# Ring depths of the one-hot and message tiles, and the iteration in which a block's end reads TensorE's results, in a two-layer graph attention and mixture-of-experts kernel

## The chip, the cores and the metric

The kernel runs on one core of one Trainium2 chip. The metric is the device time of one execution in microseconds (us); for a kernel with several runs the median is given. A core has five engines with their own instruction streams: TensorE (PE, with its weight loads shown apart as PEld), VectorE (DVE), ScalarE (ACT), GpSimd (POOL) and SyncE (SP). They wait for each other on semaphores. Here POOL issues the row gathers, SP nearly all other transfers.

## The reference, cut to what matters

There are N = 6250 nodes with 256 features and E = 206250 edges, sorted by `dst`. Two graph attention layers are followed by a mixture of 8 experts, each with a residual. A layer is

```
h = x @ W.T + b
score = (h @ a[:d])[src] + (h @ a[d:])[dst]
e = exp(-leaky_relu(score, 0.2))
h_prime = segment_sum(e[:, None] * h[dst], src, num_segments=N)
h_prime = layernorm(h_prime) * g + beta        # then elu
```

Layer 1 has 8 heads of 64 columns (512 in all), layer 2 one head of 256. The expert part takes a layernorm of the result, a router with the top 2 of 8, and for each expert `gelu(t @ w1 + b1) @ w2 + b2`, weighted and added.

## The kernel before, in words

**Stages.** First the edges are sorted into 49 blocks of 128 source nodes, while the table of layer 1 (`tab1`, a row of 512 features and 8 scores for each node) is made. Then `edges` runs layer 1, with `middle` closing each block into a row of `tab2` (256 features and a score); then `edges` runs layer 2, with `tail` closing each block and feeding the experts. A last branch, for graphs that overflow the block capacity, is not taken with these inputs.

**Groups.** A block's edges are handled in groups of GT = 5 tiles of 128 edges: 7 groups in a block, 6 in the last, so 342 groups in a layer. `edges` emits an order written out by hand. Iteration t of its loop (L587) emits, for different groups, the seven stages of the list at L579; "ahead" is how many groups before its use a stage is emitted:

- `weigh`, group t+2, on DVE: reduce the source scores from a PSUM bank `ps` into `ssum` (L541), add the gathered scores (L543), leaky relu into `lr` (L489); ACT makes `ee` of it (L490).
- `messages`, group t+1, on DVE. In layer 1 it makes `hot`, 5 one-hot matrices of 128 by 128 (L556), and `msg`, the gathered rows times `ee` (L559). In layer 2 it makes only `hot`, with `ee` multiplied in (L565, five instructions), and the gathered tile `gt` itself serves as the message.
- `source_sums`, group t+4, on PE: five small matmuls of the one-hot rows `ot` into `ps` (L536).
- `add`, group t, on PE: five matmuls of `hot` and message into the block's accumulator `acc` (L574). In f32 the profile shows each as two matmuls and two weight loads, so 10 matmul records a group.
- `one_hot`, group t+5, on DVE: `ot` (L530).
- `sources`, group t+11, on SP: the transfer of `rb` (L519).
- `gather`, 6 groups ahead in layer 1 and 8 in layer 2, on POOL: five indirect transfers into `gt` (L525).

An engine executes its own instructions in this order, so an instruction that waits holds up everything behind it on its engine.

**Rings.** A tile with `bufs=n` is written anew for group m once the last reader of group m-n is done. Before: `hot` 3, `msg` 3, `ot` 3, `gt` 6 (layer 1) or 8 (layer 2), `rb` 6, and in PSUM `ps` 2, `acc` 2, `ee` 2 and one bank `mid` in layer 1. Thus `hot` of group m waits for `add` of group m-3; `ps` of group m is made by PE once `weigh` of group m-2 has read the bank; a gather into layer 1's `gt` waits for `messages`, in layer 2 for `add`.

**Block ends.** When `add` has emitted the last group of a block at iteration t, a generator is put on the list `running` with t+2 (L596); from then on each iteration advances it to its next `yield`, after the stages of that iteration. In layer 1 its steps are: mean and centring on DVE, squares on ACT (L673 to L678); variance (L681, L682) and its root; scaling and transposes of PE into `pt2` (L685 to L690); nothing; ACT reads `pt2` (L696, L698); DVE makes `ht` (L702) and PE multiplies it into `ph2` (L705) in the same step; nothing; DVE adds the bias out of `ph2` into `row2` (L709) and SP stores it (L710). `pt2`, `ph2` and the transposes `pe` of `read_back` (L478 to L484) share the bank `mid`. In layer 2 (`tail`) the transposes of step 3 (L798) are copied by ACT two steps later (L801), the router product (L805) is read by DVE two steps after it was emitted (L809).

**Read-back.** Every 21 groups of layer 1 `read_back` loads the sorted edges of three later blocks and makes their indices; it is started at iterations with t % 21 == 0 (L588) and runs as a generator too.

Of the kernel before, what the change touches and what calls it, by code (L numbers as in the profile page):

```python
# [29 lines left out]
P = 128  # L30
ALPHA = 0.2
EPS = 1e-5
TILES = 35
GT = 5
# [12 lines left out]
def kernel(ctx: ExitStack, tc: tile.TileContext, x, src, dst, w_heads, b_heads, a_heads,  # L47
# [30 lines left out]
    RBL = 3  # L78
# [19 lines left out]
    def bank(tag, name):  # L98
        return banks["pool"].tile([P, 512], F32, tag=tag, name=name, bufs=banks["bufs"][tag])
# [392 lines left out]
    def edges(es, layer, table, sel, k, width, block_done, more=None):  # L492
# [11 lines left out]
        groups = [(b, g) for b in range(NB) for g in range(tiles[b] // GT)]  # L504
        now = [{} for _ in groups]
        accs = {}

        def tile_of(n, name, shape, bufs, dtype=F32):
            now[n][name] = eb.tile(shape, dtype, name=name, bufs=bufs)
            return now[n][name]  # L510

        def where(n):
            b, g = groups[n]
            return b, b // RBL, (b % RBL) * PITCH + g * GT
# [35 lines left out]
        def messages(n):  # L550
            b, c, t0 = where(n)
            gt, ee = now[n]["gt"], now[n]["ee"]
            hot = tile_of(n, "hot", [P, GT, P], 3)
            sl = sloc[c][:, t0:t0 + GT]
            if k > 1:
                nc.vector.tensor_tensor(hot, iota_ps[:, None, :P].to_broadcast([P, GT, P]),  # L556
                                        sl[:, :, None].to_broadcast([P, GT, P]), op=OP.is_equal)
                msg = tile_of(n, "msg", [P, GT, width], 3)
                nc.vector.tensor_mul(msg.rearrange("p j (h d) -> p j h d", h=k),  # L559
                                     gt[:, :, :width].rearrange("p j (h d) -> p j h d", h=k),  # L560
                                     ee[:, :, :, None].to_broadcast([P, GT, k, width // k]))
            else:
                now[n]["msg"] = gt
                for j in range(GT):
                    nc.vector.tensor_scalar(hot[:, j, :], iota_n, sl[:, j:j + 1], ee[:, j, :],  # L565
                                            op0=OP.is_equal, op1=OP.mult)

        def add(n):
# [8 lines left out]
            return b if g == last else None  # L577

        stages = [(weigh, 2), (messages, 1), (source_sums, 4), (add, 0), (one_hot, 5), (sources, 5 + RB), (gather, GB)]  # L579
        running = []  # L580
        t = -5 - RB
        with tc.manual_schedule():
            if layer == 1:
                for _ in read_back(eb, 0):
                    pass
                running.append((t, read_back(eb, 1)))
            while t < len(groups) or running or (more and more(len(groups))):  # L587
                if layer == 1 and 0 <= t < len(groups) and t % (RBL * TILES // GT) == 0:  # L588
                    c = groups[t][0] // RBL + 2
                    if c < NCH:  # L590
                        running.append((t, read_back(eb, c)))
                for stage, ahead in stages:
                    if 0 <= t + ahead < len(groups):
                        b = stage(t + ahead)
                        if b is not None:
                            running.append((t + 2, block_done(b, accs.pop(b)[:, :width])))  # L596
                for of in list(running):
                    if of[0] <= t and next(of[1], True):
                        running.remove(of)
                if more and t < len(groups):  # L600
                    more()
                t += 1
# [64 lines left out]
    def middle(ms):  # L667
        mw = ms.enter_context(tc.tile_pool(name="mid_w", bufs=2))

        def block_done(b, acc):  # L670
# [29 lines left out]
            yield  # L700

            nc.vector.scalar_tensor_tensor(ht, ex, 1.0, ht, op0=OP.min, op1=OP.add)  # L702
            ph = bank("mid", "ph2")
            for k in range(KH):
                nc.tensor.matmul(ph[:, :C2], ht[:, k, :], wo[:, k, :], start=(k == 0), stop=(k == KH - 1))  # L705
            yield
            yield
            row = mw.tile([P, C2], F32, name="row2")
# [6 lines left out]
    def tail(ts):  # L715
# [49 lines left out]
        def block_done(b, acc):  # L765
# [32 lines left out]
                nc.tensor.transpose(pt[:, k * P:(k + 1) * P], tok[:, k * P:(k + 1) * P], ident)  # L798
            yield
            yield  # L800
            nc.scalar.copy(tokt[:, :, i * P:(i + 1) * P], pt[:, :F].rearrange("p (k n) -> p k n", k=KF))  # L801
            yield
            pl = bank("pt", "pl")
            for k in range(KF):
                nc.tensor.matmul(pl[:, :NE], tokt[:, k, i * P:(i + 1) * P], rws[:, k, :],  # L805
                                 start=(k == 0), stop=(k == KF - 1))
            yield
            yield
            nc.vector.tensor_copy(logits[:, i, :], pl[:, :NE])  # L809
# [122 lines left out]
        def more(steps=None):  # L932
# [11 lines left out]
            return some  # L944

        return block_done, more


    with ExitStack() as es:
        psum_of("first", es, acc=2, ps=2, ee=2, mid=1, iota=1)  # L950
        edges(es, 1, tab1, sel1, H, HD, middle(es))
        pieces(es.enter_context(tc.tile_pool(name="sel2", bufs=1)), sel2, s2, 1)

    with ExitStack() as es:
        psum_of("second", es, acc=2, ps=2, ffn=3, pt=1)
        done, more = tail(es)
        edges(es, 2, tab2, sel2, 1, F, done, more)
# [70 lines left out]
```

## Time and profile before

| | |
|---|---|
| five runs, us | 5814.6, 5835.68, 5831.93, 5821.91, 5812.93 |
| median, us | 5821.91 |
| the profiled execution, us | 5818.56 |
| its span from first to last instruction, us | 5816.8 |
| mean granted TensorE clock | 0.825 |
| busy share: PE, DVE, POOL, ACT | 72%, 57%, 60%, 22% |
| edges' sort and table, about | 0 to 490 us |
| layer 1, about | 490 to 3160 us |
| layer 2 with the experts, about | 3210 to 5710 us |
| last experts, about | 5710 to 5817 us |

The busy time of an engine by itself does not say what bounds the kernel: the three large ones rest between 28% and 43% of the time, and within a stage they hand work to each other in rings. So the views to read are those of one stage: which wait ends last, and who was waited for. In a timeline the columns are the start and the duration in us, the engine, the line and operation, the tiles, the count of merged instructions, and in brackets the idle time just before with what ended it. "issue" there stands for a wait that no recorded event explains on the engine's own side, "remote" for one that no recorded event of another engine explains.

### The profile page before, as it was taken

The numbers are of one execution on the slowest core, as the hardware profiler recorded it, in microseconds if no ns is written. First come the engines' busy times: TensorE is split into PE (matmuls) and PEld (weight loads), VectorE is DVE, ScalarE is ACT, GpSimd is POOL, SyncE is SP. The second block draws the span as 40 slices with busy tenths as digits, with TensorE's granted clock in tenths as the row PEclk, the third lists the DMA queues.
The fourth block names the chain that finished last, engine by engine and source line by source line (L and its number), as shares of the span: only waits on it lengthen the run. The fifth ranks groups of instructions, "written<-read, shape, count | busy, mean of one in ns | idle before, by whom it ended". The sixth has DMA issues, their size and how long they took to land.

```text
span 5816.8 us, 55830 instructions
## 1 busy us (share of the span) xinstructions
PE 4182.6 (72%) x17929; PEld 2507.9 (43%) x17929; DVE 3300.0 (57%) x8062; ACT 1289.4 (22%) x2363; POOL 3463.4 (60%) x3570
## 2 busy tenths in 40 slices
PE   5784677776777677777767356787778777777778
PEld 4662333333333333333333234555555545555555
DVE  7874666666666666666666244444444444445443
ACT  1110111111111111111111012333334333333433
POOL 2335666666666566665664666666666666666660
PEclk8896888888878888888888667888888888888889
DMA  2115666666666666666664544444444444444440
GB/s 73 57 42 147 193 195 196 196 190 194 192 195 198 193 195 196 195 198 189 193 201 140 149 117 116 121 121 116 120 122 113 121 121 122 114 121 123 113 114 17
DMA packets 381489, 847.54 MB, mean 146 GB/s; under 512 B 90125, under 2 KB 209732, under 8 KB 381186
## 3 DMA queue, kind: packets, MB, share of 16 engines
q0 software_dynamic: 223232, 682.22, 41.8%
q1 hardware_dynamic: 150340, 155.05, 9.5%
q10 hardware_dynamic: 7614, 6.62, 0.4%
q8 instruction: 142, 2.33, 0.2%
q14 instruction: 161, 1.32, 0.1%
HBM read 814.41 MB, written 29.16 MB: 145 GB/s over the span
## 4 chain that ended last, share of the span: by engine, by line
PE 33%; DVE 20%; issue 18%; another core or an unknown queue 11%; POOL 10%; DMA 7%; DVEq 0%; ACT 0%; POOLq 0%; ACTq 0%; SPq 0%
PE acc L574 19%; POOL gt L525 10%; DVE msg L559 8%; PE ph L882 5%; PE py L890 5%; DMA srt<-run,to 5%; DMA gt<-tab,dst_idx 2%; DVE hot L565 2%; DVE hot L556 1%; DVE ot L530 1%; PE ps L536 1%; DVE ssum L541 1%; DVE ssum L543 1%; PE ph L705 1%
## 5 line engine op out<-in xcount | busy, mean ns | idle before, releaser
L525 POOL DMA_INDIRECT gt<-tab,dst_idx x3420 | 3293.0, 963 | 1901.2 <-issue 962.1
L574 PE MATMUL acc<-msg,hot 128*128 128x512 f32 x3420 | 1752.3, 656 | 208.8 <-issue 208.0
L574 PE MATMUL acc<-gt,hot 128*128 128x256 f32 x3420 | 1053.3, 450 | 223.4 <-issue 200.4
L574 PEld LDWEIGHTS acc<-msg,hot 128*128 128x128 f32 x3420 | 682.8, 208 | 991.0 <-issue 990.3
L559 DVE TENSOR_TENSOR msg<-gt,ee 128x2560 f32<-128x2560 f32 x342 | 960.6, 2809 | 0.0
L574 PEld LDWEIGHTS acc<-gt,hot 128*128 128x128 f32 x3420 | 728.3, 222 | 395.2 <-issue 278.7
L536 PE MATMUL ps<-sel,ot 128*128 128x24 bf16 (+1 forms) x3420 | 205.7, 171 | 730.6 <-issue 376.1
L490 ACT ACTIVATE ee<-lr 128x40 f32<-128x40 f32 (+1 forms) x684 | 142.1, 208 | 2426.2 <-DVE lr L489 1318.2
L536 PEld LDWEIGHTS <-ot 128*128 128x128 bf16 x3420 | 192.8, 100 | 1034.9 <-issue 846.7
L565 DVE TENSOR_SCALAR hot<-iota_n,sloc,ee 128x128 f32<-128x128 f32 x1710 | 473.6, 358 | 263.4 <-PE acc L574 147.0
L556 DVE TENSOR_TENSOR hot<-iota_ps,sloc 128x640 f32<-128x640 f32 x342 | 279.8, 818 | 542.1 <-remote 361.1
L895 DVE SCALAR_TENSOR_TENSOR xq<-py,comb,xq 128x256 f32<-128x256 f32 x392 | 170.7, 478 | 610.3 <-remote 217.8
L882 PE MATMUL ph<-tokt,w1s 128*128 128x512 f32 (+1 forms) x832 | 405.8, 612 | 36.7 <-issue 35.0
L890 PE MATMUL py<-w2s,h 128*128 128x256 f32 x1568 | 408.1, 406 | 25.3 <-issue 21.2
L490 ACT ACT_TABLE_LOAD x252 | 323.3, 1283 | 375.1 <-issue 142.8
L541 DVE TENSOR_REDUCE ssum<-ps 128x40 f32<-128x120 f32 (+1 forms) x684 | 150.6, 220 | 384.9 <-remote 270.3
L890 PEld LDWEIGHTS py<-w2s,h 128*128 128x128 f32 x1568 | 320.3, 207 | 108.4 <-issue 53.9
L262 POOL DMA_INDIRECT srt<-run,to x136 | 164.2, 1207 | 316.0 <-DMA srt<-run,to 191.8
L530 DVE TENSOR_SCALAR ot<-rb,iota_p 128x640 bf16<-128x640 bf16 x684 | 261.1, 382 | 4.4 <-DMA rb<-srow 4.4
L882 PEld LDWEIGHTS ph<-tokt,w1s 128*128 128x128 f32 x832 | 160.2, 203 | 177.9 <-issue 167.1
L705 PE MATMUL ph<-wo,ht 128*128 128x258 f32 x392 | 135.4, 500 | 129.4 <-DVE ht L702 101.1
L884 ACT ACTIVATE h<-ph,b1s 128x512 f32<-128x512 f32 (+1 forms) x208 | 135.4, 662 | 299.3 <-PE acc L574 106.4
(185 smaller groups left out, 3025.2 us busy)
## 6 DMA issues: line engine op xcount, KB each, us to landing
rb<-srow SPq DMA_DIRECT2D x684, 160.0 KB
gt<-tab,dst_idx POOLq DMA_INDIRECT x3420
tab<-row SPq DMA_DIRECT2D x49, 260.0 KB
tab<-row SPq DMA_DIRECT2D x49, 128.5 KB
xq<-in_x_dram SPq DMA_DIRECT2D x12, 512.0 KB
out_dram<-xq SPq DMA_DIRECT2D x12, 512.0 KB
xc<-in_x_dram SPq DMA_DIRECT2D x6, 896.0 KB
srt<-run,to POOLq DMA_INDIRECT x136
```

The lines of the kernel that those rows point to most:

```text
L490: nc.scalar.activation(ee, lr, AF.Exp, scale=-1.0)
L525: nc.gpsimd.indirect_dma_start(out=gt[:, j, :], out_offset=None, in_=table, in_offset=bass.IndirectOffsetOnAxis(ap=dst_idx[c][:, t0 + j:t0 ...
L530: nc.vector.tensor_scalar(tile_of(n, "ot", [P, GT * P], 3, BF16), now[n]["rb"], iota_p, None, op0=OP.is_equal)
L536: nc.tensor.matmul(ps[:, j * 3 * k:(j + 1) * 3 * k], ot[:, j * P:(j + 1) * P], sel[:, groups[n][0]].rearrange("p t k -> p (t k)"), start=T ...
L541: nc.vector.tensor_reduce(ssum, now[n]["ps"][:, :GT * 3 * k].rearrange("p (j t k) -> p j k t", j=GT, t=3), axis=AX.X, op=OP.add)
L556: nc.vector.tensor_tensor(hot, iota_ps[:, None, :P].to_broadcast([P, GT, P]), sl[:, :, None].to_broadcast([P, GT, P]), op=OP.is_equal)
L559: nc.vector.tensor_mul(msg.rearrange("p j (h d) -> p j h d", h=k), gt[:, :, :width].rearrange("p j (h d) -> p j h d", h=k), ee[:, :, :, No ...
L565: nc.vector.tensor_scalar(hot[:, j, :], iota_n, sl[:, j:j + 1], ee[:, j, :], op0=OP.is_equal, op1=OP.mult)
L574: nc.tensor.matmul(accs[b][:, :width], now[n]["hot"][:, j, :], now[n]["msg"][:, j, :width], start=(g == 0 and j == 0), stop=(g == last and ...
L705: nc.tensor.matmul(ph[:, :C2], ht[:, k, :], wo[:, k, :], start=(k == 0), stop=(k == KH - 1))
L882: nc.tensor.matmul(ph[:, :W], w1s[:, e, k, f * P:(f + 1) * P], tokt[:, k, :W], start=(k == 0), stop=(k == KF - 1))
L890: nc.tensor.matmul(py[:, (i - lo) * F:(i - lo + 1) * F], h1[:, k, i * P:(i + 1) * P], w2s[:, e, k, :], start=(k == 0), stop=(k == KF - 1))
```

## The change

The depth of `hot` becomes 4 in layer 1 and 5 in layer 2, that of `msg` 4. A block's end starts one iteration later (t+3). In `middle`, `ht` and the product into `ph2` are put into two steps, and `ph2` is read three steps after it was emitted, not two. In `tail`, the copy of the transposes and the read of the router product each come one step later. `read_back` starts at iterations with t % 21 == 5, which moves its use of the bank `mid` to where the shifted block ends leave it free. Nothing is added to or taken from the arithmetic.

```
-            hot = tile_of(n, "hot", [P, GT, P], 3)
+            hot = tile_of(n, "hot", [P, GT, P], 4 if k > 1 else 5)
...
-                msg = tile_of(n, "msg", [P, GT, width], 3)
+                msg = tile_of(n, "msg", [P, GT, width], 4)
...
-                if layer == 1 and 0 <= t < len(groups) and t % (RBL * TILES // GT) == 0:
+                if layer == 1 and 0 <= t < len(groups) and t % (RBL * TILES // GT) == TILES // GT - 2:
...
-                            running.append((t + 2, block_done(b, accs.pop(b)[:, :width])))
+                            running.append((t + 3, block_done(b, accs.pop(b)[:, :width])))
...
             nc.vector.scalar_tensor_tensor(ht, ex, 1.0, ht, op0=OP.min, op1=OP.add)
+            yield
             ph = bank("mid", "ph2")
             for k in range(KH):
                 nc.tensor.matmul(ph[:, :C2], ht[:, k, :], wo[:, k, :], start=(k == 0), stop=(k == KH - 1))
+            yield
             yield
             yield
             row = mw.tile([P, C2], F32, name="row2")
...
             yield
             yield
+            yield
             nc.scalar.copy(tokt[:, :, i * P:(i + 1) * P], pt[:, :F].rearrange("p (k n) -> p k n", k=KF))
...
                 nc.tensor.matmul(pl[:, :NE], tokt[:, k, i * P:(i + 1) * P], rws[:, k, :],
                                  start=(k == 0), stop=(k == KF - 1))
+            yield
             yield
             yield
             nc.vector.tensor_copy(logits[:, i, :], pl[:, :NE])
```

## The prediction, made before the changed kernel was run

> **What bounds the kernel now.** The two layers take 5.2 of the 5.8 ms and layer 1 alone some 2.67 ms, so I read layer 1 first, in the stretch from 700 to 3100 us (306 of its 342 groups, 2400 us, 7.84 us a group). In the groups by line the columns are busy us and mean ns of one, then the idle time just before them and what ended it:
>
> ```profile
> L574 PE MATMUL acc<-msg,hot 128*128 128x512 f32 x3062 | 1568.6, 656 | 179.2 <-issue 178.3
> L525 POOL DMA_INDIRECT gt<-tab,dst_idx x1530 | 1466.5, 958 | 928.0 <-DVE msg L559 474.4 <-issue 440.0 <-DMA gt<-tab,dst_idx 6.0
> L559 DVE TENSOR_TENSOR msg<-gt,ee 128x2560 f32<-128x2560 f32 x306 | 859.5, 2809 | 0.0
> L556 DVE TENSOR_TENSOR hot<-iota_ps,sloc 128x640 f32<-128x640 f32 x306 | 250.3, 818 | 457.7 <-remote 295.0 <-PE acc L574 97.9 <-PE ps L536 34.8
> ```
>
> POOL has no rest of its own: 1466.5 busy, 440.0 between issues (0.29 each, 1.25 us a gather, 6.24 us a group), and 474.4 in which it waits until `msg` has freed a `gt` buffer. Without that last item layer 1 would run at 6.24 us a group. So the second view is the waits of the stretch (total, times, longest):
>
> ```profile
> POOL gt L525 <- DVE msg L559: 474.4, 71, 9.2
> ...
> DVE hot L556 <- remote: 295.0, 49, 12.5
> ...
> DVE ssum L541 <- remote: 176.1, 32, 13.0
> ...
> DVE row L709 <- remote: 126.6, 17, 12.3
> ...
> PE ph L705 <- DVE ht L702: 84.7, 16, 6.7
> ```
>
> VectorE makes `msg` late because it stands at L556, L541 and L709, all of them instructions that need a result of TensorE. `msg` itself never waits (0.0). The timeline shows one such stop:
>
> ```profile
> 1515.89 0.82 DVE L556 TENSOR_TENSOR hot<-iota_ps,sloc 128x640 f32<-128x640 f32 x1 [12.52 <-remote]
> ...
> 1519.71 1.45 POOL L525 DMA_INDIRECT gt<-tab,dst_idx  x1 [7.11 <-DVE msg L559]
> ...
> 1520.39 3.43 PE L705 MATMUL ph<-wo,ht 128*128 128x258 f32 x8 [3.51 <-DVE ht L702]
> ```
>
> Counting ten L574 matmuls a group, the `hot` at 1515.89 needed the `add` whose last matmul is recorded as ended at 1500.4: its word came 15.5 us late. The stretches of that time show what TensorE did (busy us and count, then the granted clock, the DMA share and GB/s):
>
> ```profile
> 530.00:555.00 25.00, 9.10 (x10) 2.72 (x10) 0.12 (x1) 0.21 (x1) 15.98 (x17) 0.50 0.68 204
> 1490.00:1506.00 16.00, 16.00 (x60) 7.34 (x58) 13.13 (x19) 4.22 (x13) 12.11 (x13) 1.00 0.81 239
> 1506.00:1516.00 10.00, 5.53 (x7) 1.67 (x7) 0.11 (x1) 0.00 (x0) 5.07 (x6) 0.68 0.67 200
> ```
>
> From 1490 to 1506 it does 60 matmuls in 16 us; from 1506 to 1516 only 7 in 10 us, although their inputs lie ready; at the start of layer 1, 10 in 25 us. I call this a **hold**. What makes it I can't see; it occurs only while gathers run, and VectorE sits it out. The loop is: hold, VectorE stops, POOL fills its ring and stops (71 pauses of 6.68 us), the hold ends, VectorE makes a `msg`, POOL goes on. The bound is this loop, not one engine.
>
> **The change part by part.**
>
> *`hot` and `msg` 4 deep in layer 1.* No instruction is added. The order of the changed program shows that the `hot` of L556 carries no wait on TensorE any more: with 4 buffers it needs `add` of group m-4, and the L541 ahead of it on VectorE has already waited for a `source_sums` that TensorE does after that `add`. So the stop moves from L556 to the next L541: before it VectorE gets one `hot`, `msg` and `ot` further, 0.82 + 2.81 + 0.38 = 4.01 us of work done inside the hold, and POOL gets one buffer more, 6.24 us of gathers. It does not get two: `ps` keeps two banks, and L541 waits as before. Now to time. A pause comes every 306 / 71 = 4.31 groups and costs 6.68 / 4.31 = 1.55 us a group. If 49 of the 71 runs of gathers (those that end at L556) become a group longer, a run has 5.0 groups. The restart gets slower there: the L541, L543 and L489 (0.27 + 0.20 + 0.20 = 0.68 us) now come after the hold; 0.69 of them, so a pause of 7.15 us and 1.43 us a group. 342 x 0.12 = **-41 us**. Bounds: at best all pauses go, -474.4 x 342/306 = -530 us; at worst the longer run only lengthens the hold, +162 (worked out under the last rival).
>
> *`row2` read three steps after `ph2`.* By the same order rule L709 falls behind an L541 that waits for something later, so its 17 stops merge with those of L541. Such a stop costs POOL 8.59 us (from 1479.1 to 1487.7) where the one above cost 7.11: 17 x 1.5 x 1.12 = **-28 us** (0 to 126.6 x 1.12 = -141).
>
> *`ht` a step ahead of its product.* TensorE no longer runs into a product whose `ht` VectorE has still to make: 84.7 us named and 23.6 "issue" before L705. Most of this lies in a pause anyway: of the 3.51 us shown, from 1516.9 to 1520.4, 0.7 come after POOL went on at 1519.7. I count that fifth: 108 x 1.12 x 0.2 = **-24 us** (0 to -121).
>
> *Block ends an iteration later, read-back at 5.* The accumulator ring is two blocks deep: block b is read at its last group plus 3 and its bank wanted at plus 8, so nothing waits for it. `read_back` has 24 iterations of slack at its old place; on SP its two loads and its store pass five `rb` transfers, which are themselves issued 11 groups ahead. The shared bank fits: `pe` at iterations 6 to 7 of 7, `ph2` from 1 to 4, `pt2` from 4 to 6. Nothing, with the slack as cover; were it gone, a load as at the start of the layer (issued at 494.56, waited for until 497.39), 2.8 us, 16 times, +45 us. Only for the last block, which has 6 groups, does `pt2` now wait for the `row2` before it; no group is left by then, and the two lie in one chain anyway: nothing, or the 0.42 us of a `row2`.
>
> *Layer 2: `hot` 5 deep, two reads later.* Here `gt` is freed by `add`, so POOL gains nothing directly. The waits from 3300 to 5700:
>
> ```profile
> POOL gt L525 <- PE acc L574: 127.8, 58, 4.2
> ...
> PE ps L536 <- DVE ssum L541: 117.6, 28, 10.7
> ```
>
> VectorE stands 234.9 us at `hot` (L565), but 559 at the experts' `xq` (L895), 164 at L541, 104 at L876 and 98 at L869, which stay; 234.9 is a fifth of the 1160 in all. What TensorE waits for VectorE, 117.6 us, falls by that fifth: **-24 us** (0 to -118). The two later reads take away waits of 8.3 and 11.1 us that others cover: 0 to -19, I count nothing. ACT's order loses 14 table loads of 1.28 us; ACT is busy 22%: nothing.
>
> *The end.* The experts of a batch start three iterations later; at 1.5 steps each 4.5 steps of 1.9 us (eight L890 matmuls take 1.89) fall behind the last group, 0 to +9; TensorE has as many fewer before it, so half: **+5 us**.
>
> Sum: -41 - 28 - 24 - 24 + 5 = -112 us. The profiled execution took 5818.56 us (span 5816.8), so 5707; it lies 3 us under the median of the runs, 5821.91, so about **5710 us**.
>
> [...] The row first: 59 records of TensorE lie between the matmul that VectorE waited for at 1515.89 and the last one issued by then. [...] Next row: the granted clock is 0.50 from 530 to 555 and 0.68 from 1506 to 1516. [...]
>
> **The rivals.** *The reach is worth its full time.* All 74 stops at L556 (49, and 25 put down to other events, 457.7 us together) pay 4.01 us, 332 us over the layer with the factor 1.12, less the L541 stops that grow, so some -250 in all: **5570**. For it: VectorE never waits for a gather (6.0 us of DMA behind POOL's own row), so it sets POOL's pace. Against: in the 25 us before 554.88 POOL did run, and TensorE did 10 matmuls.
>
> *Nothing moves.* POOL pauses because TensorE, not VectorE, is behind: it does so much between holds, and a longer ring fills once and stays full. Within 17 us of **5815**. For it: TensorE is 72% busy and leads the chain that ended last with 33%.
>
> *Slower: the hold grows with the run of gathers.* In the first hold of the layer POOL had six free buffers and ran until 550.9; VectorE's stop ended only at 554.88, 25.00 us long, against 12.52 with POOL stopped at 1512.6. A run one group longer is 6.24 us more of hold, in which TensorE does 2 or 3 matmuls (10 in 25 us), not the 10 of a group. If a third of the 71 x 1.12 = 79 pauses of the layer comes with a hold grown so and no group gained, 26 x 6.24 = +162, less the 52 of `row2` and `ht`: up to +110; with half of that **5870**. It decides as soon as the groups per pause stay at 4.3 while the stops get longer.
>
> ```profile
> 554.88 0.82 DVE L556 TENSOR_TENSOR hot<-iota_ps,sloc 128x640 f32<-128x640 f32 x1 [25.00 <-remote]
> ```
>
> **How the numbers follow.** The sum 0.42 (5650 to 5790), full reach 0.15 (5500 to 5650), nothing 0.14, slower 0.29 (5840 to 5960). 0.3% or 17 us is about what a measurement of this kernel can tell from no change. Faster 0.57, same 0.14, slower 0.29. The range 5590 to 5890 leaves out half of the full reach and a third of the slower case, 0.17.
>
> **What would show it.** In the changed profile from 700 to 3100 us: L556 idle near 0 and L541 more than its 200 us, L709 near 0 (sure; otherwise the change does not do what it says). POOL's wait for `msg`: 5 groups a pause in the sum, under 300 us in all for full reach, 4.3 groups a pause in the other two. L705's wait gone. Wrong if L541's stops take all that L556 gives up, with 20 us and more among them: then the hold follows the gathers.

## The result and the profile after

The changed kernel took 5835.65 us (median of 26 runs, 5824.31 to 5852.23), the kernel before 5825.98 us (median of 47, 5811.35 to 5850.48): ratio 1.0016, 95% interval 1.0008 to 1.0024. That is 0.16% slower, with an interval clear of 1, though under the 0.3% that the prediction took for no change. The forecast of 5710 us, 112 us faster, was wrong: the measured time lies within its range of 5590 to 5890 us, but on the other side of the kernel before. To read the numbers further down it must be known that the kernel before takes 4.97 ms on core 0 of some chips and 5.82 to 5.88 ms on core 0 of others. The profiled execution took 5828.69 us (span 5826.8, granted clock 0.823).

The groups by line of the changed kernel, 700 to 3100 us, with the columns of before (busy us, mean ns | idle before, what ended it):

```profile
L574 PE MATMUL acc<-msg,hot 128*128 128x512 f32 x3073 | 1611.5, 666 | 283.9 <-issue 283.5
L525 POOL DMA_INDIRECT gt<-tab,dst_idx x1537 | 1473.1, 958 | 928.0 <-DVE msg L559 465.0 <-issue 447.5 <-DVE hot L556 11.0
...
L556 DVE TENSOR_TENSOR hot<-iota_ps,sloc 128x640 f32<-128x640 f32 x308 | 251.4, 816 | 0.0
...
L541 DVE TENSOR_REDUCE ssum<-ps 128x40 f32<-128x120 f32 x307 | 84.5, 275 | 757.9 <-remote 647.7 <-issue 50.2 <-PE ps L536 31.9
...
L711 DVE TENSOR_TENSOR row<-ph,bo 128x258 f32<-128x258 f32 x44 | 18.3, 417 | 0.0
```

And its waits in the same stretch (total, times, longest):

```profile
DVE ssum L541 <- remote: 647.7, 56, 14.7
POOL gt L525 <- DVE msg L559: 465.0, 66, 9.5
```

Every wait that was to go has gone: L556 and `row2` (now L711) stand at 0.0, the product's wait for `ht` is no longer listed. But VectorE stood 457.7 + 200.0 + 133.2 = 790.9 us at L556, L541 and `row2` before, and now stands 757.9 us at L541 alone. The two rows of the kernel before that the prediction does not show:

```profile
L541 DVE TENSOR_REDUCE ssum<-ps 128x40 f32<-128x120 f32 x306 | 83.9, 274 | 200.0 <-remote 176.1 <-issue 18.7 <-PE acc L574 3.2
...
L709 DVE TENSOR_TENSOR row<-ph,bo 128x258 f32<-128x258 f32 x44 | 18.5, 419 | 133.2 <-remote 126.6 <-PE acc L574 6.7
```

POOL makes 66 pauses instead of 71, of 7.05 us instead of 6.68: 465.0 us against 474.4.

Counting POOL's gaps of over 2 us between gathers over the whole of layer 1, there were 78 of 6.69 us before (521.8 in all) and 69 of 7.53 us after (519.7). Layer 1 takes 2662.8 us from its first gather to its last before, 2663.1 after; layer 2 2471.9 and 2468.9. The 10.0 us by which the span is longer lie between the layers (51.9 to 54.9) and behind the last gather (135.6 to 145.5).

### The profile page after: what moved, and what is told of

Its sections match the earlier page's. It is cut to its first block, busy times and chain, and to the rows that moved or that the text cites. A ratio compares the mean times of both kernels' runs of the same rounds, so it can differ in the third digit from the quotient of the medians.

```text
span 5826.8 us, 55626 instructions
## 1 busy us (share of the span) xinstructions
PE 4189.0 (72%) x17929; PEld 2484.1 (43%) x17929; DVE 3294.5 (57%) x8062; ACT 1270.6 (22%) x2349; POOL 3458.6 (59%) x3570
## 4 chain that ended last, share of the span: by engine, by line
PE 31%; issue 20%; DVE 17%; POOL 14%; another core or an unknown queue 10%; DMA 6%; ACT 0%; DVEq 0%; POOLq 0%; ACTq 0%; SPq 0%
PE acc L574 16%; POOL gt L525 14%; DVE msg L559 7%; PE py L894 6%; PE ph L886 6%; DMA srt<-run,to 5%; DVE hot L565 1%; DVE hot L556 1%; DMA gt<-tab,dst_idx 1%; DVE ot L530 1%; PE ps L536 1%; DVE ssum L541 1%; DVE ssum L543 1%; DVE lr L489 1%
## 5 line engine op out<-in xcount | busy, mean ns | idle before, releaser
L574 PE MATMUL acc<-msg,hot 128*128 128x512 f32 x3420 | 1792.0, 665 | 320.9 <-issue 320.5
L574 PE MATMUL acc<-gt,hot 128*128 128x256 f32 x3420 | 1034.7, 443 | 247.0 <-issue 233.7
L574 PEld LDWEIGHTS acc<-msg,hot 128*128 128x128 f32 x3420 | 690.2, 210 | 1133.8 <-issue 1133.6
L559 DVE TENSOR_TENSOR msg<-gt,ee 128x2560 f32<-128x2560 f32 x342 | 960.7, 2809 | 0.0
L574 PEld LDWEIGHTS acc<-gt,hot 128*128 128x128 f32 x3420 | 713.3, 218 | 427.3 <-issue 325.5
L541 DVE TENSOR_REDUCE ssum<-ps 128x40 f32<-128x120 f32 (+1 forms) x684 | 151.3, 221 | 1181.5 <-remote 932.3
L899 DVE SCALAR_TENSOR_TENSOR xq<-py,comb,xq 128x256 f32<-128x256 f32 x392 | 171.3, 478 | 701.9 <-remote 307.1
L565 DVE TENSOR_SCALAR hot<-iota_n,sloc,ee 128x128 f32<-128x128 f32 x1710 | 474.8, 356 | 26.7 <-ACT ee L490 21.6
L556 DVE TENSOR_TENSOR hot<-iota_ps,sloc 128x640 f32<-128x640 f32 x342 | 279.2, 816 | 0.0
```

The lines of the kernel that those rows point to most:

```text
L541: nc.vector.tensor_reduce(ssum, now[n]["ps"][:, :GT * 3 * k].rearrange("p (j t k) -> p j k t", j=GT, t=3), axis=AX.X, op=OP.add)
L574: nc.tensor.matmul(accs[b][:, :width], now[n]["hot"][:, j, :], now[n]["msg"][:, j, :width], start=(g == 0 and j == 0), stop=(g == last and ...
```

## The experiments

The theory that I took from this, **balance**: TensorE falls behind while gathers run and catches up in POOL's pauses, so a deeper ring buys a longer run and a longer pause. Against it stood **next ring** (`ps` with two banks is now what binds VectorE) and **the parts cancel** (rings gain, later reads lose, or the other way round). Each experiment is told with its chip, and with the kernel before on that chip. The edits are cut to the lines that matter, with constants filled in.

### Four kernels on a chip where the kernel before takes 4.97 ms (chip 11)

`e1_rings`, the rings alone:

```
-hot = tile_of(n, "hot", [P, GT, P], 3)
+hot = tile_of(n, "hot", [P, GT, P], 4 if k > 1 else 5)
-    msg = tile_of(n, "msg", [P, GT, width], 3)
+    msg = tile_of(n, "msg", [P, GT, width], 4)
```

> The rings of hot and msg alone, 4 deep in layer 1 and hot 5 deep in layer 2; the reads of block ends as before. Theory 'balance' (TensorE falls behind while gathers run and catches up only in POOL's pauses, so a longer run of gathers buys a longer pause): within 17 us of the kernel before, the runs of gathers longer (4.6 to 5.0 groups), the pauses longer (7.2 to 7.6 us), their sum in layer 1 still 500 to 540 us. Rival 'the parts cancel' (the rings gain their 41 + 24 us and the later reads lose as much): 30 to 65 us faster.

`e2_reads`, all the rest of the change (the edit is against the changed kernel):

```
-hot = tile_of(n, "hot", [P, GT, P], 4 if k > 1 else 5)
+hot = tile_of(n, "hot", [P, GT, P], 3)
-    msg = tile_of(n, "msg", [P, GT, width], 4)
+    msg = tile_of(n, "msg", [P, GT, width], 3)
```

> The later reads of block ends, the ht step and the moved read-back alone; rings as before. 'Balance': within 17 us of the kernel before, L705's wait for ht gone (from 85 us to near 0), POOL's pauses in layer 1 still 500 to 540 us in the sum. 'The parts cancel': 30 to 60 us slower if the rings gain, 30 to 60 us faster if the rings lose.

`e3_gb4`, from the changed kernel:

```
-GB = 6 if k > 1 else 8
+GB = 4 if k > 1 else 8
```

> The changed kernel with four gt buffers in layer 1 where it has six. 'Balance': runs of gathers a group or two shorter and pauses shorter in the same measure, so the sum stays and the time is within 40 us of the changed kernel's, until the ring is too short to cover the 7 us from a gather to its msg. Rival 'the ring sets it' (each pause costs its 6.7 us whatever the run is, so shorter runs mean more pauses): runs of 3 groups, pauses 1.67 times as many, some 300 us slower.

`e4_reach`, from the changed kernel (`hot` and `msg` also become 6 deep and `ot` 5):

```
-psum_of("first", es, acc=2, ps=2, ee=2, mid=1, iota=1)
+psum_of("first", es, acc=2, ps=4, mid=1, iota=1)
-    ee = now[n]["ee"] = bank("ee", "ee")[:, :GT * k].rearrange(...)
+    ee = tile_of(n, "ee", [P, GT, k], 3)
-stages = [..., (source_sums, 4), (add, 0), (one_hot, 5), (sources, 5 + RB), ...]
+stages = [..., (source_sums, 6), (add, 0), (one_hot, 7), (sources, 7 + RB), ...]
```

> The changed kernel with the next wait lifted too: four ps banks (ee goes to SBUF), source_sums and one_hot two iterations earlier, hot and msg 6 deep, ot 5 deep in layer 1. Rival 'next ring' (VectorE stops at L541 because ps has two banks; two more groups of reach are 8 us of its work inside each hold): L541's idle time in layer 1 falls from 758 to under 300 us and the kernel is 150 to 300 us faster. 'Balance': L541 idles as long as before in the sum, in fewer and longer stops; runs of gathers of 6 groups and more, pauses of 9 us and more, time within 30 us of the changed kernel.

Measured, against 4967.04 us there: e1_rings 4970.69 us, ratio 1.0007 (0.9998 to 1.0016); e2_reads 4982.15, 1.0031 (1.0019 to 1.0043); e3_gb4 4981.75, 1.003 (1.0019 to 1.0041); e4_reach 5696.61, 1.1466 (1.1449 to 1.1482).

None of these says what it was made for, because here there is nothing to explain: POOL never pauses for over 2 us in either layer, and VectorE never waits for TensorE. No theory foresaw that. The groups of the kernel before on such a chip (`c_before` below, 700 to 2600 us):

```profile
L525 POOL DMA_INDIRECT gt<-tab,dst_idx x1514 | 1439.1, 951 | 461.2 <-issue 436.8 <-DMA gt<-tab,dst_idx 16.5 <-DVE hot L556 3.7
L574 PE MATMUL acc<-msg,hot 128*128 128x512 f32 x3029 | 1435.0, 624 | 0.0
...
L541 DVE TENSOR_REDUCE ssum<-ps 128x40 f32<-128x120 f32 x302 | 82.9, 275 | 0.0
```

POOL issues without a rest, 1900 us for 303 groups, 6.27 us a group: the 6.24 us that the prediction gave for layer 1 without pauses. The matmuls of L574 have no idle time ahead of them and L541 none either. The same program has no hold on this chip.

e4_reach tells something else. It moved `ee` from PSUM to SBUF, so that `msg` (L557 there) has both inputs in SBUF, and a gather of POOL now takes 1379 ns in the mean (700 to 2500 us) instead of some 950. Its timeline:

```profile
1501.67 2.81 DVE L557 TENSOR_TENSOR msg<-gt,ee 128x2560 f32<-128x2560 f32 x1
1502.03 3.27 POOL L526 DMA_INDIRECT gt<-tab,dst_idx  x1 [0.30 <-DVE hot L554]
```

The gather that starts while L557 runs ends 0.82 us after it, 3.27 us instead of 0.95. That is the price of this edit (5697 against 4982 us; layer 1's gathers sum to 2353.5 us, against 1632.1 in e3_gb4), and the test of the reach was lost in it; h4_reach below makes it with `ee` kept in PSUM.

### The two kernels themselves, no gathers, slower gathers (chip 2)

> The kernel before once more, for its profile beside the runs of this call: on the chip of the first profile 5.82 ms with 500 to 540 us of POOL's pauses in layer 1 and TensorE's holds; on the chip of the four experiments above 4.97 ms, without pauses and holds. Where the chip alone makes the difference, one of these two pictures comes back whole, with layer 1 at 7.8 or at 6.3 us a group and nothing between.

> The changed kernel on the same chip. On a chip with holds 'balance' expects a ratio of 1.000 to 1.003, as measured; on a chip without holds VectorE never stops for TensorE, so rings and later reads have nothing to gain, and the ratio is that of the later reads alone there, 1.002 to 1.004. Rival 'the rings pay where no hold lengthens with them': on a chip without holds 0.995 or less.

`e5_nogather`, from the changed kernel, leaves out the gathers of layer 1 after the first six groups, so that layer 1 computes something else with the same work:

```
+if k > 1 and n >= GB:
+    now[n]["gt"] = kept[n % GB]
+    return
```

> The changed kernel with the gathers of layer 1 left out after the first six groups: every group uses one of the six gathered buffers, so what layer 1 computes is wrong, its work on TensorE, VectorE and ScalarE the same. 'Gathers make the holds': on any chip no hold in layer 1, TensorE never 10 matmuls in 25 us, layer 1 at VectorE's or TensorE's own pace, 5.0 to 5.6 us a group instead of 7.8 or 6.3. Rival 'the hold is TensorE's own' (its clock or its instruction supply): on a chip with holds they stay, layer 1 at 6 us a group and more.

`e8_pace128`, from the changed kernel (`rest` is a tile of 128 by 128):

```
 for j in range(GT):
+    if k > 1:
+        nc.gpsimd.memset(rest, 0.0)
```

> The changed kernel with a memset of 128 columns (206 ns by the row of ident) on POOL ahead of each gather of layer 1: 1.45 to 1.6 us a gather instead of 1.25, 7.3 to 8.0 us a group without any pause. On a chip with holds, 'the rate makes the hold': the holds go, POOL's waits for msg fall under 100 us and layer 1 takes 7.3 to 7.8 us a group, 0 to 180 us faster than the changed kernel. 'Time since the pause makes it' (a hold 19 us after POOL goes on, whatever the rate): the pauses stay, 1 us a group and more, 200 to 400 us slower. On a chip without holds both expect 342 x 1.0 to 1.7 us, 340 to 580 us more than there.

Measured, against 4970.52 us: c_before 4967.67 us (one run), c_after 4984.3, ratio 1.0026 (1.0014 to 1.0037); e5_nogather 4592.13 and e8_pace128 5150.68 (one run each). Again no hold, so the picture with 6.3 us a group came back whole, and c_after's ratio is that of the later reads. Without gathers the adds of layer 1 take 1755 us, 5.13 us a group: this is what TensorE and VectorE need by themselves. The memset cost 166 us and not 340 to 580: 0.097 us a gather, the rest of its 227 ns lies in the 0.30 us between two gathers.

The loss of 0.3% where there are no holds can be followed. From c_before to c_after the span grows by 17.7 us: POOL's gathers of layer 1 sum to 1634.9 us instead of 1625.1, and from the last gather to the end it is 124.6 us instead of 118.3. The gathers first. Taking 0.95 us for one, from 700 to 2600 us 17 gathers that ran beside L686 were longer before, by 2.7 us together; after the change 36, by 11.1 us; these 8.4 us more are most of the 9.8. One of them in c_after:

```profile
1476.09 0.69 DVE L686 TENSOR_TENSOR hc<-hc,rs 128x512 f32<-128x512 f32 x1
1476.19 1.41 POOL L525 DMA_INDIRECT gt<-tab,dst_idx  x1 [0.30 <-issue]
```

L686 too has two inputs in SBUF. The block ends now meet POOL's gathers at another place, and this is what it costs.

### Is it the neighbours, or the place? (chip 13)

The kernel before on two and on eight cores at once, with `core_ids=list(range(2))` and `list(range(8))`, each core computing the whole.

> The kernel before, the same program on two cores of the chip at once (each computes the whole). Theory 'neighbour' (the holds of the first profile come from other traffic on the chip beside the core that was measured): holds come back in part or whole, between 5.1 and 5.9 ms, POOL waiting for msg in layer 1. Rival 'chip' (they are a matter of that one chip, or of the time of the measurement): within 1% of the time on one core, 4.97 ms on a chip without holds.

> The kernel before on all eight cores at once. 'Neighbour': holds as in the first profile on most cores, layer 1 at 7.5 us a group and more, slowest core 5.7 ms and more, with POOL's pauses of 6 to 8 us. 'Chip': no holds; some per cent more than 4.97 ms at most, from lower granted clocks or longer gathers, without POOL waiting for msg.

Measured: 6073.16 us for e9_two (one run), with core 0 at 5811.5 and core 1 at 6071.3; the kernel before alone took 5822.77. The company of a second core leaves core 0 as it was. e9_eight took 6375.55 us (median of 3); the spans by core of the profiled one, and the granted clock:

```profile
core 0: 6100.4 us, clock 0.800
core 1: 6306.1 us, clock 0.792
core 2: 5871.2 us, clock 0.809
core 3: 6071.5 us, clock 0.802
core 4: 5071.7 us, clock 0.882
core 5: 4959.9 us, clock 0.891
core 6: 5046.8 us, clock 0.883
core 7: 4936.7 us, clock 0.890
```

On one chip, in one execution, cores 0 to 3 run with holds and cores 4 to 7 without. From 700 to 2600 us core 0 has 54 waits of POOL for `msg` (426.7 us), cores 1 to 3 have 56 to 60; core 4 has seven (2.3 us), cores 5 to 7 six to ten. In all three executions cores 0 to 3 took 5871 us or more and cores 4 to 7 at most 5133. Neither theory held: core 0 has its holds without neighbours, cores 4 to 7 have none beside seven of them, and "the chip" is too coarse; it is a matter of which cores of which chip.

### What makes a hold (chip 10, on core 0 with holds)

These four run on two cores at once, 0 and 4 by their code; the numbers are core 0's, whose kernel before has spans of 5874.1 to 5892.9 (median 5881.0). The other core, listed as core 1, had holds as well in the three kernels with gathers, and was some 200 us longer there.

`h4_reach`, from the changed kernel (`hot` and `msg` also become 5 deep and `ot` 4):

```
-psum_of("first", es, acc=2, ps=2, ee=2, mid=1, iota=1)
+psum_of("first", es, acc=2, ps=4, mid=1, iota=1)
-    ee = now[n]["ee"] = bank("ee", "ee")[:, :GT * k].rearrange(...)
+    ee = now[n]["ee"] = now[n]["ps"][:, 256:256 + GT * k].rearrange(...)
-stages = [..., (source_sums, 4), (add, 0), (one_hot, 5), (sources, 5 + RB), ...]
+stages = [..., (source_sums, 5), (add, 0), (one_hot, 6), (sources, 6 + RB), ...]
```

> The changed kernel with the next wait lifted: ps and ee of a group share a PSUM bank, so there are four of them, source_sums and one_hot come one iteration earlier, hot and msg are 5 deep, ot 4 deep in layer 1; ee stays in PSUM. It runs on core 0 and on core 4 at once (each the whole problem); the spans of the cores are compared, core 0 with the kernel before on core 0. On a core with holds, rival 'next ring': L541's 758 us of idle time in layer 1 fall by a quarter and more, 60 to 250 us faster than the changed kernel. 'Balance': within 30 us of it, the runs of gathers longer by half a group to a group, the pauses longer by as much as makes their sum the same, 500 to 560 us in layer 1. On a core without holds: within 15 us of the changed kernel.

Measured: spans of 5923.2 to 5928.3 on core 0 (four runs), 5924 / 5881 = 1.007. The whole program's ratio of 1.0413 (1.0392 to 1.0434) is that of the other core. POOL's pauses in layer 1: 69 of 8.19 us, 565.3 in all, just over the 560 that balance allowed. One more group of reach at every ring made the pauses longer and no fewer. **Next ring falls.**

`h5_nogather` is e5_nogather on the two cores.

> The changed kernel without the gathers of layer 1 after the first six groups (every group uses one of these six, so layer 1's result is wrong and its work on the other engines the same), on cores 0 and 4. On a core with holds, 'gathers make the holds': none in layer 1, which takes 1755 us from the first add to the last as on the other chip (5.13 us a group), instead of 2674. Rival 'the hold is TensorE's own' (instruction supply, clock): holds remain, 2000 us and more. On a core without holds 1755 us again.

Measured: 4944.4 us on core 0. The adds of layer 1 take 1758.6 us, against 1755 without holds on chip 2, and from 700 to 2250 us:

```profile
700.00:2250.00 1550.00, 1477.02 (x5072) 691.73 (x5071) 1518.92 (x2389) 330.20 (x818) 0.00 (x0) 1.00 0.17 37
```

TensorE 95% busy, granted clock 1.00; VectorE 98% busy. The transfers that are left, most of them the `rb` loads on SP's queue (160 KB a group), still move 37 GB/s. **The gathers make the holds**, and nothing is wrong with TensorE by itself.

`h6_free`, from the changed kernel, lets the gathers run into buffers that nobody reads, so that layer 1 computes something else here too:

```
+if k > 1 and n >= 2:
+    now[n]["gt"] = kept[n % 2]
+    gt = eb.tile([P, GT, row], F32, name="gx", bufs=4)
```

> The changed kernel in which layer 1's gathers all run, but from the third group on into buffers that nobody reads (the groups use the first two gathered buffers, so layer 1's result is wrong, the work of the engines the same): POOL never waits for msg. Cores 0 and 4. On a core with holds, 'gathers make the holds, POOL's pauses end them': POOL needs 6.3 us a group, 2150 us in all, and TensorE falls far behind, at 0.4 to 1 record a us where it needs 33.6 a group; it gets through less than half of its groups by the last gather, and layer 1 ends 700 us and more after it. Rival 'the loop makes them' (holds come from what VectorE and TensorE wait for each other, not from the traffic): layer 1 takes 2150 to 2250 us. On a core without holds 2150 to 2200 us.

Measured: 6756.5 us on core 0. POOL was not quite free: it waits for `dst_idx`, which VectorE makes late. So it runs 131 us and stands 89 us, over and over (15 stands in all, 1270.8 us). Two stretches, one with gathers, one mostly without (busy us and count of TensorE, its weight loads, VectorE, ScalarE, POOL; granted clock, DMA share, GB/s):

```profile
1500.00:1600.00 100.00, 26.17 (x36) 7.86 (x36) 9.48 (x13) 3.32 (x10) 66.69 (x71) 0.50 0.76 198
1600.00:1700.00 100.00, 94.09 (x312) 43.66 (x311) 92.53 (x148) 19.60 (x46) 17.21 (x19) 0.97 0.29 76
```

Layer 1 takes 3570 us from its first add to its last, where it takes 2674 in the first profile; the last add comes 180 us after the last gather and not 700, because of these stands. 36 matmuls in 100 us with gathers, 312 without, although no engine needs what these gathers bring. The loop between VectorE and POOL isn't needed for a hold. A pause isn't needed to let a word through either, only to let it through soon: L541 waited up to 49.4 us for one.

`h8_pace` is e8_pace128 on the two cores.

> The changed kernel with the memset of 128 columns ahead of each gather of layer 1, on cores 0 and 4; without holds it cost 166 us (0.096 a gather: 1.35 us a gather, 6.75 a group). On a core with holds, 'the rate makes the hold': POOL's pauses fall from 520 to under 250 us in layer 1 and the time is 0 to 150 us under the changed kernel's. 'TensorE has only so much room while gathers run': it needs 33.6 records a group and does them at a rate that the slower gathers leave alone, so pauses shrink by what the gathers grow, within 60 us of the changed kernel. 'Time since the pause': pauses as before, 130 to 200 us slower.

Measured: 5859.2 us on core 0 (one run), 22 less than the kernel before. Pauses 55 of 6.39 us, 351.5 in all, 168 less than in the first profile of the changed kernel; POOL's other gaps 657 us instead of 505. What POOL loses by the memsets it gains in pauses: within the 60 us of *room*, and no threshold between these two rates.

### Parts, TensorE's work, and shallower rings (chip 6, core 0 with holds)

`g1_rings` and `g2_reads` are e1_rings and e2_reads once more.

> The rings alone once more (hot and msg 4 deep in layer 1, hot 5 deep in layer 2, block ends as before), on one core, for a core with holds. 'Balance': within 17 us of the kernel before, pauses fewer and longer, 500 to 540 us in layer 1. The prediction's own step: 65 us faster. Rival 'the parts cancel': 30 us faster and more. On a core without holds 0.9998 to 1.0016 again.

> The later reads alone once more, on one core, for a core with holds. 'Balance', with the 15 us that they cost on a core without holds (longer gathers beside L686, a later end): 5 to 20 us slower than the kernel before, pauses in layer 1 500 to 540 us, L705's wait gone. The prediction's own steps (row2, ht, the end): 47 us faster. On a core without holds 1.002 to 1.004 again.

`g3_bf16`, from the changed kernel (`msg` is rounded to bf16, `hot` is exact in it):

```
-hot = tile_of(n, "hot", [P, GT, P], 4 if k > 1 else 5)
+hot = tile_of(n, "hot", [P, GT, P], 4 if k > 1 else 5, BF16 if k > 1 else F32)
-    msg = tile_of(n, "msg", [P, GT, width], 4)
+    msg = tile_of(n, "msg", [P, GT, width], 4, BF16)
```

> The changed kernel with hot and msg of layer 1 in bf16 (msg is rounded, the sums stay f32), so that L574 is 5 matmuls and 5 weight loads a group instead of 10 and 10: 23 records of TensorE a group instead of 33. On a core with holds, 'room' (TensorE does some 3.7 records a us while gathers run and the rest in the pauses): 23 records need no more than the 6.25 us of a group's gathers, pauses in layer 1 fall from 520 to under 150 us, 300 to 500 us faster. Rival 'a hold is a span of time' (a fixed stop of 10 to 20 us, whatever TensorE has to do): pauses fall by less than a third, 50 to 170 us faster. On a core without holds, where POOL's gathers set layer 1: within 30 us of the changed kernel.

`g4_two`: the changed kernel with `hot` and `msg` 2 deep in layer 1.

> The changed kernel with hot and msg only 2 deep in layer 1. On a core with holds 'balance': the runs of gathers shorter and the pauses shorter, so within 40 us of the changed kernel, POOL's pauses 500 to 560 us in layer 1. The prediction's step turned round (0.7 group less of run for each buffer, two buffers): 80 to 130 us slower. On a core without holds within 30 us of the changed kernel.

Measured, against 5825.4 us: g1_rings 5855.65 us, ratio 1.0046 (1.0029 to 1.0062); g2_reads 5825.36, 0.999 (0.9973 to 1.0008); g3_bf16 5793.95, 0.9938 (0.9918 to 0.9958); g4_two 5922.02, 1.0167 (1.0136 to 1.0197). POOL's pauses in layer 1, with those from above:

| hot and msg deep | kernel | pauses | us each | sum us |
|---|---|---|---|---|
| 2 | g4_two | 96 | 6.07 | 582.3 |
| 3 | before | 78 | 6.69 | 521.8 |
| 3, later reads | g2_reads | 80 | 6.52 | 521.4 |
| 4 | g1_rings | 72 | 7.83 | 564.1 |
| 4, later reads | after | 69 | 7.53 | 519.7 |
| 5, ps 4, later reads | h4_reach | 69 | 8.19 | 565.3 |

Up to four deep, each buffer makes the pauses fewer and longer; the fifth (with the other rings, on chip 10) makes them only longer. g4_two's loss, 97 us, is about what the prediction's step turned round expected; it is from 3 to 4 that the step fails. From 2 to 3 the fewer win by 61 us, from 3 to 4 the longer win by 42, and with the later reads it comes out even. "The parts cancel" is true on a core with holds, the other way round from what I had tested for: it is the rings that lose (1.0046 alone), and with the later reads beside them the loss is smaller (1.0016, in another set of runs), while the later reads alone gain nothing that can be told. In g1_rings the waits of 700 to 3100 us:

```profile
DVE ssum L541 <- remote: 690.9, 58, 16.0
POOL gt L525 <- DVE msg L559: 511.2, 68, 13.3
```

g3_bf16 brings *room*, and with it balance, down: 31 us faster than the kernel before and not 300 to 500, and 459.7 us of pauses in layer 1 left of 520. It is less even than the rival for a fixed span allowed (50 to 170). In that stretch TensorE was busy 838.05 us instead of 1748.13, and its waits there:

```profile
PE ps L536 <- DVE ssum L541: 850.2, 108, 21.8
DVE ssum L541 <- remote: 695.9, 49, 19.7
```

TensorE is far ahead, waits for VectorE, and VectorE waits for TensorE, at the same time. One such stop, in the timeline:

```profile
1484.71 1.11 PE L690 MATMUL pt<-ident,hc 128*128 128x128 f32 x4 [3.16 <-issue]
...
1485.62 0.33 PE L536 MATMUL ps<-sel,ot 128*128 128x24 bf16 x5
...
1511.38 0.46 ACT L696 ACTIVATE ht<-pt,bet,gam 128x128 f32<-128x128 f32 x1 [21.30 <-remote]
...
1512.13 0.28 DVE L541 TENSOR_REDUCE ssum<-ps 128x40 f32<-128x120 f32 x1 [18.59 <-remote]
...
1512.46 0.29 PE L536 MATMUL ps<-sel,ot 128*128 128x24 bf16 x5 [21.77 <-DVE ssum L541]
```

The `ps` that L541 needs was ended at 1485.95, the `pt` that ScalarE needs at 1485.82. Both hear of it at 1511.4 to 1512.1, some 26 us later. The trace's own record of TensorE's semaphore has updates at 1511.35, 1512.11 and 1512.21, and none between 1488.26 and these (it keeps 188 of the 232 that TensorE makes from 700 to 2200 us). From 1493 on TensorE does nothing (busy us and count of TensorE first):

```profile
1493.00:1509.00 16.00, 0.00 (x0) 0.10 (x1) 0.54 (x2) 0.00 (x0) 10.54 (x12) 0.50 0.76 225
1509.00:1512.00 3.00, 0.00 (x0) 0.00 (x0) 0.00 (x0) 0.62 (x2) 0.00 (x0) 0.50 0.13 37
```

POOL's last gather before it ended at 1506.90, its last DMA packet at 1509.99; 1.4 us after that ScalarE goes on. So a hold is not work that TensorE is behind with. **TensorE's words, the semaphore updates that say a result is there, arrive late while gathers move data**; here three come through within 0.9 us once the traffic has stopped. The stop that the prediction shows, at 1515.89 in the kernel before, fits: the record of the same semaphore has four updates from 1515.87 to 1516.11, and the work that they would tell of ended at 1500.40, 1500.51, 1504.90 and 1505.02. One limit: the ends of matmuls are modelled in the profile, so it does not tell a late word from a result that is itself late. Over groups 10 to 329, from the later of the end of `source_sums` and the end of VectorE's instruction ahead, to L541 (the last column counts those before which no packet of a gather had begun for 1 us):

| kernel | L541 over 3 us late | mean | longest | traffic stopped |
|---|---|---|---|---|
| c_before (no holds) | 0 | | | |
| h5_nogather (core with holds) | 0 | | | |
| after | 70 | 11.1 | 14.7 | 35 |
| g3_bf16 | 51 | 14.3 | 19.7 | 42 |
| h6_free | 55 | 28.7 | 49.4 | 16 |

So a word often comes when the traffic stops, but where it goes on for 131 us, as in h6_free, most come, later, while it runs.

Words from VectorE to ScalarE and back are not late in these kernels: from `lr` to `ee` it takes 0.09 us in the median and 0.4 at most, and `msg` starts as soon as VectorE is free for it. In the f32 kernels the slow records of TensorE come on top; with a bf16 `add` they are gone (in 700 to 3100 us, TensorE's records that wait for no semaphore and start over 0.6 us after the one ahead have 2 us of idle time ahead of them in all, 572 in the changed kernel), and the stops remain.

The trace itself thins out at the same places. From 700 to 2200 us it holds 602 of the 1473 updates that VectorE's instructions make of VectorE's semaphore in the kernel before, 633 of 1481 in the changed one and 535 of 1510 in g3_bf16, but 1816 of 1821 in c_before, 2245 of 2245 in h5_nogather, and in e9_eight 596 of 1396 on core 0 against 1767 of 1771 on core 4. In layer 1 of the changed kernel it has 447 of 461 in the first 4 us after POOL goes on, 128 of 504 in the next 4 us, and all 232 from 4 us into a pause on. VectorE's words themselves were in time; what is lost is their record. So records are lost on the cores, and in the stretches, in which TensorE's words are late. Each run here comes with a span and a granted clock of its own, so each was recorded. A rival stands that no run excludes: that it is the recording, together with the gathers, that holds TensorE back on these cores, and that without it the kernel takes another time there.

g3_bf16 is also the one version that beats both kernels where there are holds, by 0.6% against the kernel before; half of TensorE's adds are worth so little because they were not what was waited for. It was not run on a core without them.

## Why the prediction was wrong

- **The bound.** The loop was read rightly: hold, VectorE stops, POOL fills its ring and stops, the hold ends. "The bound is this loop, not one engine" stands, on cores with holds. That the hold occurs "only while gathers run" was all that the profile could show; h5_nogather and h6_free make the gathers a cause of it, without showing how they do it.
- **`hot` and `msg` 4 deep, -41 us: the step that failed.** "4.01 us of work done inside the hold" took the length of a hold as given, so that the run of gathers would grow by a group and the pause by 0.47 us. The stops did move to L541 as said. But the hold goes on with the gathers: the runs grew to 4.65 groups a pause (307 / 66) from 4.31, not to 5.0, while the pause grew to 7.05 us, near the 7.15 forecast; over the whole layer the pauses sum to 519.7 us instead of 521.8. Alone the rings made the pauses sum to 564.1 us and cost 0.46%, some 27 us, inside the range of -530 to +162 but on its other side. In the loop the reach sets how far POOL runs before it stops, and POOL's stop is what lets TensorE's words through soon (L541 waits at most 14.7 us in the changed kernel, up to 49.4 in h6_free, where the gathers go on for 131): the work that VectorE wins inside it is paid for with a longer one.
- **`row2`, -28 us, and `ht`, -24 us.** The mechanism was right: L709's stops and L705's wait are gone. The size was not: in g2_reads L556 and L541 stand 601.1 + 152.3 = 753.4 us where the three lines stood 790.9, and POOL's pauses stay at 521. An interval of -16 to +5 us holds neither these terms nor their sum.
- **Block ends and read-back at nothing.** No wait was added, as argued. But the working looked at waits alone. Where no hold hides it, the gathers take 9.8 us more, most of it at the new place of L686 beside them.
- **Layer 2, -24 us.** Its gathers take 2468.9 us instead of 2471.9. The 263.4 us at L565 went (26.7 now, in the whole run) and came back in front of L541 (340.7 in layer 2 instead of 176.9) and of the experts' `xq` (701.9 instead of 610.3). Counted at -3.
- **The end, +5 us (0 to +9).** 9.9 us in the profiles here, 6.4 on the chip without holds. The one term of the right sign, though twice its size and a little over its bound; it is nearly all of the measured difference.
- **Rivals.** *Nothing moves* came nearest (5835.65 is 21 us over its 5815, which was to hold within 17; 5840 is where *slower* begins), but not by its reason: it has TensorE behind with its work, and with half of that work (g3_bf16) the pauses still sum to 459.7 us. *The hold grows with the run of gathers* had the mechanism, shown by g1_rings, h4_reach and h6_free; it was sized at up to +162 for the rings, +110 with the later reads, and cost 27 for the rings alone. *Full reach* falls with h4_reach; its 74 stops at L556 are 75 in the trace.
- **What would show it.** The condition for wrong, "L541's stops take all that L556 gives up", came about; stops of 20 us did not, the longest is 14.7.
- **The 59 records and the granted clock.** No run shows that the 59 records between result and stop had a part in the late word. In the stop of g3_bf16 31 records lie behind the `ps` (15 matmuls and 16 weight loads), the work that the late words tell of is done by the record, TensorE stands idle behind it (no matmul from 1493 to 1509), and L541 stands 719.5 us in the stretch: there it was not work still to be done that made the word late. The granted clock is low in the stops (0.68 from 1506 to 1516 in the kernel before, 0.50 from 1493 to 1512 in g3_bf16). But g3_bf16 had a granted clock of 0.57 in the stretch against 0.83 before and was faster: the low clock does not set the time there.

What stays open: why gathers hold back TensorE's words on some cores and not on others, and what starts a hold some time after POOL goes on. The lost records hint that more than TensorE's words is held up there, and whether the recording is part of the cause is not tested. Nor was it tried to carry TensorE's word in another way.

## What to carry to other kernels

Before you deepen a ring, find out whether the word that ends the wait is late because its engine is late, or late by itself: halve the producer's work and see whether the wait shrinks. Where the thing that holds you up lasts as long as your own traffic, a deeper ring can let the traffic run longer and gain nothing: from 2 to 3 buffers the pauses shrank by 61 us here, from 3 to 4 they grew by 42. Fewer crossings between the engines in question would be the next thing to try; no run here did. And profile on more than one core and chip: a stretch that cost 2663 us here is 2146 us elsewhere, and the change is worth something else there. Count the records too: where a trace misses many, ask what the recording does to the time.

## What the runs showed of the hardware

- The same program takes 4.97 ms on core 0 of chips 2 and 11 and 5.82 to 5.88 ms on core 0 of chips 6, 10 and 13; with all eight cores of chip 13 at work, 4.94 to 5.07 ms on cores 4 to 7 and 5.87 to 6.31 on cores 0 to 3 in the execution shown. In c_before (chip 2) L541 is never over 3 us late over groups 10 to 329 of layer 1; with holds it is, 70 times in the changed kernel, 51 in g3_bf16 (chip 6), 55 in h6_free (chip 10).
- Beside a VectorE instruction with both inputs in SBUF a gather of POOL took longer: 3.27 us instead of 0.95 beside L557 (2.81 us, e4_reach) and 1.41 beside L686 (0.69 us, c_after). With `ee` in PSUM L559 leaves the gathers at 0.95 (c_before).
- On a core with holds the trace loses VectorE's semaphore updates while gathers run (633 of 1481 kept in the changed kernel from 700 to 2200 us) and none without gathers (2245 of 2245, h5_nogather).
- The 37 GB/s that h5_nogather still moves, most of it `rb` loads on SP's queue, held no word back: L541 is never over 3 us late there.
